# Three rearrangements in a hybrid scan, attention and feed-forward kernel: load order at the start, place of the sums and bias of the first blocks, and where an output product is cut

## The chip, the cores and the metric

The kernel runs on one core of a Trainium2 chip. The metric is the device time of one execution in microseconds (us); lower is better. Several executions are timed and their median is compared. One more execution is recorded by the hardware profiler; its own time lies beside those of the timed runs, and its rows are what the text below reads. A core has five engines that run side by side, each with its own queue of instructions: TensorE (PE in the profile, with PEld for its weight loads), VectorE (DVE), ScalarE (ACT), GpSimd (POOL) and SyncE (SP). They wait for each other through semaphores. Sixteen DMA engines move data; they are fed by queues of SP, ACT and POOL.

## What is computed

The input `x` is 2 sequences of 2048 rows of 256 floats. Four residual stages follow one another, each on normalised rows:

```python
x = x + attn_a(_layernorm(x))   # a gated scan over time
x = x + ffn(_layernorm(x))
x = x + attn_b(_layernorm(x))   # a second-order linear attention, 16 heads of 64
x = x + ffn(_layernorm(x))      # the same weights as the first feed-forward part
```

`attn_a` normalises once more with a gain `gamma`, multiplies by `w_qkva` (256 to 3 x 256: the parts q, kv and a), takes the sigmoid of a, runs `s_t = a_t * s_(t-1) + kv_t` along time, and returns `q * s`. `ffn` rounds both weight matrices to three values around a scale that is the mean of their absolute values (w + (t - w), so the result is -1, 0 or 1), and computes `gelu(x W1 + b1) W2 + b2`. `attn_b` keeps running sums over time of k k', q v' and a product of both, and ends in an output product with `W_o` (1024 to 256). All is in float32.

## The kernel before

All rows of `x` stay in SBUF for the whole kernel, as `x_sb`: 32 chunks of 128 rows. Four chunks are a block (512 rows, 512 KB), and `blocks` lists the eight blocks with the two sequences in turn, so `blocks[0]` is chunks 0 to 3 and `blocks[1]` chunks 16 to 19. The engines' orders (PE, DVE, ACT, POOL) are written out by hand: an engine issues its instructions in the order in which the Python code makes them, and waits in that order.

**Loads (L110 to L143).** SP and ACT share the four chunks of block 0, then ACT takes `gam` (1 KB, 8 bytes for each partition), and SP takes `wqkva` in three parts of 256 KB: part 2 (a), 1 (kv), 0 (q). Then SP loads block 1 (L117), the two halves of `w1` (L119), block 2 (L120), `w2` (L121), the other blocks (L123) and the attention's weights (L125). POOL's queue loads `b1_sb` (L142, 4 KB) and `b2_sb` (L143), which is one row of 1 KB copied to all 128 partitions (128 KB).

**The front (L680 to L903).** Block 0 is scanned in two units of two chunks (units 0 and 1), each further block is one unit (unit 2 is block 1). For a unit u: `s_(u)` makes the statistics of its rows on DVE (L156, L157, L165, L166) and ends them on POOL (L169, L173, L174); `r_(u)` normalises rows (L183 on DVE for units 0 and 1, L188 on ACT later); `t_(u)` turns them by PE transposes (L212) and copies with the gain on ACT (L216); `q_(u, e)` multiplies a half e of the features on PE (L334: part a, then kv, then q, one PSUM bank each), takes the sigmoid on ACT (L343), runs the scan on DVE (L353), copies the last column on POOL (L355) and multiplies by q on DVE (L357); `a_(u)` turns the result back (L433) and adds it to `x_sb` (L435). There are eight PSUM banks, taken in turn, so a product waits until the reader of the product eight banks ago is done. Between these steps the weights of the feed-forward part are rounded: `ternary_part` has two DVE instructions (L322, L323) and one on POOL (L324) for a quarter of a matrix. The first lines of the order are:

```python
s_(0, bias=False); r_(0); s_(1, bias=False); r_(1); t_(0); q_(0, 0); s_(2); t_(1); q_(0, 1)
```

Then a loop over the blocks, with index i, runs the feed-forward part of block i (`ffn_in`: L532 on PE, L544, L550 and L564 on ACT, L558 to L581 on DVE; `ffn_out`: L623, L629), and between its products the scan of a later block as seven products instead of eight (`scan_seven`: L392 on PE, L398 on DVE, L404 to L427 on ACT). `ffn_rows` on POOL (L509 to L512) makes sums that the products need. At the end of a turn i, `ffn_bias(blocks[i + 1])` adds `b2_sb` to the rows of the next block on POOL (L667), and the statistics of later blocks follow. Block 0 gets its bias at the end of turn 1.

**The attention (L913 to L1332).** It has 32 steps s (16 chunks of two sequences). In a step PE runs `inter` (L1054: queries times state), `products` (L1037, masked on DVE at L1043), the output product `outward` of an earlier step (L1115: eight matmuls into one bank; the profile counts two instructions for each), `intra` (L1068, which reads what L1043 wrote), the products that make k, q and v of the next chunks (L978, L983) and `update` (L1094). `outward(s - 2, 0)` is the last thing in step s and has the first four of its matmuls; `outward(s - 2, 1)` comes in step s + 1, between `products` and `intra`, has the other four, and DVE then adds the bank to `x_sb` (L1121). The last stage (L1451 on) is the feed-forward part once more.

## Time and profile before

| what | value |
|---|---|
| timed runs | 1212.58, 1214.03, 1215.69 us; median 1214.03 |
| the profiled execution | 1215.55 us, of it 1213.7 us from the first to the last instruction (the span) |
| granted TensorE clock | 0.999 of full |
| PE busy | 1197.3 us (99% of the span) |
| DVE, ACT, POOL busy | 818.1, 619.6, 252.3 us (67%, 51%, 21%) |
| DMA moved | 113.00 MB |
| start to 100 us, PE busy by stretch | 0 to 8.58: 5.18; 8.58 to 23.54: 14.63 of 14.96; 23.54 to 58: 34.46 of 34.46; 58 to 100: 40.85 of 42.00 us |
| 330 to 1030 us (the attention), PE busy | 693.51 of 700 us |

A row of the profile names an engine, the source line, what is written and read, and the sizes; a timeline row begins with the start and the duration in us, and ends, where the engine stood idle before it, with the idle time and what ended it. Matmuls overlap in the engine's pipeline, so two starts in a row tell more of the pace than the durations do.

### The profile page before, as it was taken

The numbers are of one execution on the slowest core, as the hardware profiler recorded it, in microseconds if no ns is written. First come the engines' busy times: TensorE is split into PE (matmuls) and PEld (weight loads), VectorE is DVE, ScalarE is ACT, GpSimd is POOL, SyncE is SP. The second block draws the span as 40 slices with busy tenths as digits, with TensorE's granted clock in tenths as the row PEclk, the third lists the DMA queues.
The fourth block names the chain that finished last, engine by engine and source line by source line (L and its number), as shares of the span: only waits on it lengthen the run. The fifth ranks groups of instructions, "written<-read, shape, count | busy, mean of one in ns | idle before, by whom it ended". The sixth has DMA issues, their size and how long they took to land.

```text
span 1213.7 us, 46646 instructions
## 1 busy us (share of the span) xinstructions
PE 1197.3 (99%) x21156; PEld 972.3 (80%) x21156; DVE 818.1 (67%) x1322; ACT 619.6 (51%) x979; POOL 252.3 (21%) x383
## 2 busy tenths in 40 slices
PE   8999999999999999999999999999999999999998
PEld 6598999999667777777778777777777889999997
DVE  7968777875567567666666656766766655676764
ACT  4356765543554554554544445445455553555542
POOL 3664335451200110110011011011011111322330
PEclk9999999999999999999999999999999999999999
DMA  9211111110244233234323323323323631212111
GB/s 319 85 61 36 35 36 35 37 56 14 88 124 135 80 125 125 91 107 134 122 82 126 123 90 125 123 92 107 124 90 107 190 96 52 70 61 79 53 52 36
DMA packets 80439, 113.00 MB, mean 93 GB/s; under 512 B 8272, under 2 KB 65360, under 8 KB 79984
## 3 DMA queue, kind: packets, MB, share of 16 engines
q1 hardware_dynamic: 77712, 105.94, 26.4%
q10 hardware_dynamic: 2448, 3.93, 1.1%
q8 instruction: 166, 2.72, 1.0%
q0 software_dynamic: 80, 0.14, 0.1%
q14 instruction: 33, 0.27, 0.1%
HBM read 58.59 MB, written 51.38 MB: 91 GB/s over the span
## 4 chain that ended last, share of the span: by engine, by line
PE 94%; DVE 2%; ACT 1%; issue 1%; POOL 1%; DMA 1%; SPq 0%; DVEq 0%; ACTq 0%; POOLq 0%
PE hy L1115 10%; PE ox L623 9%; PE hx L532 9%; PE hkN_X L983 5%; PE hp L1037 5%; PE hqT_X L978 5%; PE hvN_X L983 5%; PE oz L623 5%; PE hz L532 4%; PE huT L1068 3%; PE hS L1094 3%; PE huT L1054 3%; PE hoT L1054 3%; PE hoT L1068 3%; PE pq L334 3%; PE hM L1094 3%
## 5 line engine op out<-in xcount | busy, mean ns | idle before, releaser
L1043 DVE TENSOR_TENSOR p<-hp,mask 128x512 f32<-128x512 f32 x128 | 82.1, 682 | 96.2 <-PE hp L1037 96.2
L935 POOL TENSOR_TENSOR S<-xnT 128x128 f32<-128x128 f32 x32 | 14.8, 461 | 530.9 <-ACT xnT L280 513.2
L1115 PE MATMUL hy<-wo,oT 128*128 128x256 f32 x512 | 123.7, 385 | 0.1
L188 ACT ACTIVATE xn<-x_sb,nb,rs 128x256 f32<-128x256 f32 x124 | 65.8, 592 | 87.0 <-POOL nb L174 87.0
L1115 PEld LDWEIGHTS hy<-wo,oT 128*128 128x128 f32 x512 | 93.6, 190 | 19.2 <-issue 7.0
L544 ACT ACTIVATE hT<-hT,b_sb 128x256 f32<-128x256 f32 x192 | 85.4, 501 | 33.4 <-DVE hT L576 30.5
L1079 ACT COPY uT<-huT 128x512 f32<-128x512 f32 x32 | 18.8, 586 | 130.8 <-PE huT L1068 130.8
L1104 DVE TENSOR_TENSOR S<-S,hS 128x512 f32<-128x512 f32 x60 | 41.3, 688 | 44.5 <-PE hS L1094 41.4
L232 DVE STREAM_TRANSPOSE sqkT<-kN 128x1024 f32<-128x1024 f32 x32 | 65.8, 2058 | 1.3 <-ACT kN L1014 1.2
L1134 ACT COPY kT<-rawkT 128x1024 f32<-128x1024 f32 x32 | 66.6, 2080 | 0.0
L232 DVE STREAM_TRANSPOSE squN<-uT 128x1024 f32<-128x1024 f32 x31 | 63.6, 2051 | 4.0 <-ACT uT L1081 3.5
L1134 ACT COPY uN<-rawuN 128x1024 f32<-128x1024 f32 x31 | 64.6, 2083 | 1.6 <-DMA rawuN<-dsquN 1.2
L509 POOL TENSOR_TENSOR xT<-xnT 128x256 f32<-128x256 f32 x15 | 16.8, 1122 | 178.7 <-ACT xnT L280 118.3
L156 DVE BATCH_NORM_STATS2 st<-x_sb 128x6 f32<-128x256 f32 x128 | 51.5, 403 | 2.3 <-DMA x_sb<-in_x_dram 2.3
L1094 PEld LDWEIGHTS hS<-kN 64*64 64x64 f32 x1984 | 32.7, 134 | 23.2 <-issue 23.1
L1014 ACT COPY vN<-hvN_X 128x512 f32<-128x512 f32 x16 | 9.4, 587 | 80.0 <-PE hvN_X L983 80.0
L988 DVE TENSOR_TENSOR kN<-kN,hkN_Y 128x512 f32<-128x512 f32 x16 | 11.0, 688 | 54.7 <-ACT kN L997 54.7
L629 DVE TENSOR_TENSOR x_sb<-x_sb,ox 128x256 f32<-128x256 f32 x64 | 26.5, 414 | 30.1 <-PE ox L623 30.1
L169 POOL TENSOR_TENSOR rs<-rs,mhalf 128x2 f32<-128x2 f32 (+1 forms) x43 | 38.9, 904 | 29.4 <-DVE rs L166 26.6
L615 DVE TENSOR_TENSOR hS<-hT 128x512 f32<-128x512 f32 x62 | 41.2, 686 | 5.6 <-ACT hT L544 5.6
L334 PE MATMUL pq<-xnT,wqkva 128*128 128x512 f32 (+1 forms) x120 | 42.9, 510 | 1.4 <-DMA wqkva<-in_wqkva_t_dram 1.4
L1104 DVE TENSOR_TENSOR M<-M,hM 128x512 f32<-128x512 f32 x60 | 41.0, 684 | 4.6 <-PE hM L1094 1.4
(300 smaller groups left out, 3024.5 us busy)
## 6 DMA issues: line engine op xcount, KB each, us to landing
dsqkT<-sqkT SPq DMA_DIRECT2D x32, 512.0 KB, 3.5
rawkT<-dsqkT SPq DMA_DIRECT2D x128, 128.0 KB, 3.0
dsquN<-squN SPq DMA_DIRECT2D x31, 512.0 KB, 3.3
rawuN<-dsquN SPq DMA_DIRECT2D x124, 128.0 KB, 3.3
out_dram<-x_sb SPq DMA_DIRECT2D x16, 256.0 KB, 2.2
x_sb<-in_x_dram SPq DMA_DIRECT2D x7, 512.0 KB, 8.9
dsqxn<-sqxn SPq DMA_DIRECT2D x14, 256.0 KB, 3.7
rawxn<-dsqxn SPq DMA_DIRECT2D x56, 64.0 KB, 2.4
```

What stands on the lines that cost most here:

```text
L232: nc.vector.transpose(to, src)
L334: nc.tensor.matmul(pq[:, :nt], lhsT=wqkva[:, d, col : col + P], rhs=xnT[:, d, :], start=(d == 0), stop=(d == ND - 1),)
L532: nc.tensor.matmul(at[a][:, j, :], lhsT=A[:, f * P : (f + 1) * P], rhs=Bm, start=(new and j == 0), stop=True, skip_group_check=True,)
L544: nc.scalar.activation(out, out if src is None else src[:, j, :], AF.Gelu, bias=b1_sb[:, f : f + 1])
L623: nc.tensor.matmul(banks[name][:, c, :], lhsT=A[f // 2][:, f % 2, c * P : (c + 1) * P], rhs=Bm[:, f, :], start=(new and c == 0 and f == 0) ...
L983: nc.tensor.matmul(to, lhsT=self.A[i], rhs=self.B[i], start=new, stop=True, skip_group_check=True)
L1043: nc.vector.tensor_tensor(d[s][nm][:, h], banks[h], mask8, ALU.mult)
L1054: nc.tensor.matmul(banks[c][halves[h ^ c], p, :], lhsT=d[s][sums][c][halves[h], p, :], rhs=d[s]["qT"][halves[h], p, halves[c]], start=(p = ...
L1094: nc.tensor.matmul(banks[c][halves[h], p, :], lhsT=d[s][left][halves[c], feats(h, p)], rhs=d[s][right][halves[c], feats(h, p)], start=True ...
L1104: nc.vector.tensor_tensor(t, prev, banks[c], ALU.add)
L1115: nc.tensor.matmul(py, lhsT=d[s]["oT"][:, p, :], rhs=wo[:, p, :], start=(p == 0), stop=(p == NPR - 1),)
L1134: act(t, d[s]["r" + nm].rearrange("p t q -> p q t"))
```

## The change

There are five edits. (1) SP issues `wqkva` part 2 right after the first chunk of block 0, then the third chunk, then parts 1 and 0; ACT issues the second chunk, `gam`, and then the fourth chunk. Before, all four chunks went ahead of `gam` and `wqkva`. (2) `b2_sb` moves from POOL's queue at the start to SP's queue, behind the last rows of `x` and ahead of the attention's weights. (3) `s_(2)` stands ahead of `q_(0, 0)`: on DVE the statistics of block 1 now come before the scan of unit 0's first half; on POOL their end comes before the column copy of that scan. (4) The POOL instruction of the third quarter of `w2` (L324) is held back until `fw_(0)` (L509 to L512) has been issued, and the bias of blocks 1 and 0 is added in turn 1, after the fourth product of its `ffn_in`, in place of the ends of turns 0 and 1. (5) `outward` is cut into three and five matmuls.

```diff
     for c in range(BC):
         g = blocks[0] + c
         (nc.scalar if c % 2 else nc.sync).dma_start(out=x_sb[:, g, :], in_=xf[g * P : (g + 1) * P, :])
-    nc.scalar.dma_start(out=gam, in_=gamma)
-    for part in (2, 1, 0):
-        cols = slice(part * D, (part + 1) * D)
-        nc.sync.dma_start(out=wqkva[:, :, cols], in_=wqkva_t[:, cols].rearrange("(c p) e -> p c e", p=P))
+        if c == 1:
+            nc.scalar.dma_start(out=gam, in_=gamma)
+        if c != 1:
+            cols = slice((2, 2, 1, 0)[c] * D, ((2, 2, 1, 0)[c] + 1) * D)
+            nc.sync.dma_start(out=wqkva[:, :, cols], in_=wqkva_t[:, cols].rearrange("(c p) e -> p c e", p=P))
...
     for g0 in blocks[3:]:
         nc.sync.dma_start(out=x_sb[:, g0 : g0 + BC, :], in_=rows(xf, g0, BC))
+    nc.sync.dma_start(out=b2_sb, in_=b2.partition_broadcast(P))
...
-    nc.gpsimd.dma_start(out=b2_sb, in_=b2.partition_broadcast(P))
...
-    def ternary_part(pool, w, scale, part, name):
+    def ternary_part(pool, w, scale, part, name, later=False):
...
+        if later:
+            return lambda: nc.gpsimd.tensor_tensor(wf, wf, t, ALU.subtract)
         nc.gpsimd.tensor_tensor(wf, wf, t, ALU.subtract)
...
         t_(0)
+        s_(2)
         q_(0, 0)
-        s_(2)
         t_(1)
...
-        tern(w2, scales[2], 2)
+        rest_of = tern(w2, scales[2], 2, later=True)
         ft_(0)
         q_(4, 1)
         fw_(0)
+        rest_of()
         tern(w2, scales[2], 3)
...
                 run(squares)
                 run(steps, 2)
+                if i == 1:
+                    ffn_bias(blocks[1])
+                    ffn_bias(blocks[0])
...
-            if more:
+            if more and i > 0:
                 ffn_bias(blocks[i + 1])
-                if i == 1:
-                    ffn_bias(blocks[0])
...
-            for p in range(half * NPR // 2, (half + 1) * NPR // 2):
+            for p in range(3) if half == 0 else range(3, NPR):
```

More of the change, by code (lines that the diff above doesn't have):

```diff
@@ L720, in fw_, with tern @@
             fn[i] = ffn_rows(ffn_pool, blocks[i], fn[i])
-        def tern(w, scale, part):
-            ternary_part(tern_pool, w, scale, part, "w1" if w is w1 else "w2")
+        def tern(w, scale, part, **kw):
+            return ternary_part(tern_pool, w, scale, part, "w1" if w is w1 else "w2", **kw)
         scales = {}
```

## The prediction

> **What bounds the kernel now.** The page first: TensorE is the bound, at full clock, and every microsecond to be had is one in which it stands still.

> ```profile
> span 1213.7 us, 46646 instructions
> ...
> PE 1197.3 (99%) x21156; PEld 972.3 (80%) x21156; DVE 818.1 (67%) x1322; ACT 619.6 (51%) x979; POOL 252.3 (21%) x383
> ```

> Then PE's waits (line, what it waited for, total, times, longest):

> ```profile
> PE pq L334 <- DMA wqkva<-in_wqkva_t_dram: 1.4, 1, 1.4
> ...
> PE qax L392 <- DVE a L398: 0.8, 1, 0.8
> ...
> PE hx L532 <- POOL xT L510: 0.4, 1, 0.4
> PE hx L532 <- ACT hT L564: 0.3, 1, 0.3
> ```

> All four lie in the first 103 us, where four of the five edits are. The chain that ended last, cut to 0 to 110 us (start, us, what), says what stands behind them:

> ```profile
> 1.66 6.79 DMA wqkva<-in_wqkva_t_dram
> ...
> 14.71 1.02 POOL rs L169
> 16.87 1.58 ACT xn L188 x3
> ...
> 58.58 1.10 POOL w L324
> 59.98 0.69 POOL xT L509
> ...
> 91.58 1.41 DVE rs L165
> ```

> So: the load of part a until 8.45 us; the statistics of block 1 (end on POOL, then ACT's normalised rows); L324 ahead of L509; one small DVE instruction of 1.41 us. The change touches each. The attention has no such wait; its timeline, at one step:

> ```profile
> 572.71 0.59 ACT L1014 COPY qT<-hqT_X 128x512 f32<-128x512 f32 x1 [1.43 <-PE hqT_X L978]
> ...
> 574.33 1.16 PE L1054 MATMUL huT<-qT,S 64*64 64x64 f32 x64
> ...
> 576.36 1.99 PE L1115 MATMUL hy<-wo,oT 128*128 128x256 f32 x8
> 576.48 1.29 DVE L1043 TENSOR_TENSOR p<-hp,mask 128x512 f32<-128x512 f32 x2 [1.57 <-PE hp L1037]
> 578.28 1.31 PE L1068 MATMUL huT<-p,kN 64*64 64x64 f32 x62
> ```

> **Cutting the output product 3 and 5: nothing.** One matmul is two PE instructions 0.216 us apart, 0.43 us, moved past L1054 and L1037; no work is added. What it would cover: L1068 waits for L1043, which ends at 576.48 + 1.29 = 577.77; L1068 starts at 578.28, 0.51 us later, so there is nothing to cover. What it uncovers: L1054 starts 0.43 us earlier and needs ACT's L1014, done at 573.30; 1.03 us of room becomes 0.60. The mask's bank for L1037 has over 2 us. DVE's L1121 comes when the eighth matmul ends, as before. Bounds: a gain if the pace of these eight matmuls hides a wait (1.92 us to the next start here, 1.82 for the other half at the step's end: 0.10 x 29 steps = 3 us), against 0.43 x 30 = 13 us if the room were gone. The 0.10 sits behind the first matmul, where PE passes from 64x64 to 128x128 tiles, and that passage stays. I take 0.

> **Bias out of turn 0: 0.9 us gained.** In turn 0 POOL's L667 runs from 90.59 to 92.96; DVE's L165, 0.17 us elsewhere, starts at 91.58 and ends at 92.98, with L667. Behind it on DVE stand the two adds L398 (93.09, 93.43), and PE's fourth `qax` needs the first. Without L667 there, L165 ends at 91.75, L166 at 91.95, the adds at 92.4 and 92.7 at the latest, and PE's instruction is free when its predecessors are out: 91.88 + 4 x 0.216 = 92.74 instead of 93.66. Gain 0.92. ACT follows PE here (its L427 waits for PE), so the 0.3 us wait of L532 on L564 stays. In the new place two L667 (2.37 each) follow the norm ends of turn 0, about 99 to 104. DVE has L262, L558, L572, L576 there; other L262 beside POOL rows take 1.12 to 1.13 against 1.07 us, and L629, the first DVE add on block 1's rows, comes at 111. POOL's next work is at 113. At worst each L262 is held until an L667 ends, 1 to 2 us, and a few tenths reach PE; I take 0 for the place, 0.92 in all (0.5 to 0.95).

> **L324 behind `ffn_rows`: 0.14 us gained.** L509 now starts at 59.94, behind L324 (58.58 to 59.85). Without it the next thing in POOL's order is the column copy L355, which needs the scan L353 on DVE, 58.35 + 1.27 = 59.62. So L509 comes at 59.80, not at 58.6: 0.14. The PE wait it ends is longer, 61.85 - 60.43 - 0.86 = 0.56, and that is the upper bound. Behind it, POOL ends the w2 sums one L324 (1.25 us) later, near 71; PE reads the first of them at 73.36, 7 us after it was ready.

> **The first loads and the order of statistics and scan: 1.1 us gained.** PE's first product waits for part a until 8.58; ACT's half of `xnT` for it was ready at 7.45. With part a second on SP's queue, ahead of 512 KB that now precede it, it should be in by 4.5 to 6.8 us (below), so PE starts at 7.45, 1.13 us earlier. That gain is kept only if the next gate moves as well. On DVE block 1's statistics now stand before the first scan, and PE's unit-1 products need the bank that this scan reads; all of DVE is queued behind a transfer. Call S the start of these statistics. From the rows 11.95 to 19.92 of DVE's timeline: statistics 2.53, scan and multiply 0.79 + 0.34, the second pair the same, L290 2.31, its total 0.18, so the next scan at S + 7.28 (ACT's sigmoid for it is ready at S + 6.9); then 0.78 + 0.34 + 2.54 for block 2's statistics and 0.33 + 0.41 for the two adds L435: S + 11.7. PE's way through ACT's L188 gives the same end: those rows depend on S through POOL's L169, and 23.54 - 11.95 = 11.6. The product at 23.54 needs the second L435. Gain there: 23.54 - 11.7 = 11.85 - S. After it, to 58 us, PE is never idle and waits have 1.5 us of room, so this carries.

> S is the later of 9.57 (DVE free) and block 1's landing. Before, that was 3.52 + 8.2 = 11.7 us. Ahead of it go the same bytes but for `b2`, 128 KB. The DMA view gives 315 GB/s from 2.5 to 4 us, 166 from 4 to 6, 229 from 6 to 8, and 375 from 8 to 12. The dip is in the stretch in which `gam`'s 128 packets of 8 bytes and then `b2`'s packets of 4 KB run. [...] By the row, 6 to 8 us moved 0.46 MB in 2 us; without b2's 0.13 MB and at 375 GB/s the rest takes 0.88 us: 1.1 us sooner, S = 10.6, gain 1.25. I take S = 10.75, nearer to the row, since the neighbouring stretch shows that rate: gain 1.1, range 0.3 (`gam`'s dip grows, as now a row chunk stands behind it) to 2.2 (S = 9.6).

> The fourth chunk's wait: behind `gam` on ACT's queue. `gam` came 2.4 us after the last chunk before (6.7 against 4.3), so the chunk lands near 3.5 + 2.4 + 0.5 = 6.4 us, 7.4 at the late end; DVE wants it at 7.02. Even 7.4 moves only `r_(1)`, which ends at 9.57 and would end at 9.95, still before S. Behind it SP's second `w1` load is issued near 6.5, not 4.7 (it reuses `gam`'s semaphore); L290 needs it only at S + 4.8 = 15.5, and it landed at 14.3. On POOL the issue of `b2` (0.58 us at 2.72) goes away, ahead of 1.2 us of idle time: nothing; the column copy L355 now comes behind the statistics' end at S + 4.4, and the scan that reads it at S + 7.3. `b2` itself is needed at 99 us; the attention's weights behind it, 0.4 us later, after 300.

> **Sum.** 1.1 + 0.14 + 0.92 + 0 = 2.2 us off the profiled 1213.7 us span (1215.55 us with 1.8 around it). The median of the timed runs is 1.5 us under that execution; the difference is applied to it: 1214.03 - 2.2 = 1211.8 us, 0.18% faster. A measurement of this kernel tells about 0.3% (3.6 us) from no change; the three runs differ by 3.1.

> **Rivals.**
> 1. *The load moves but its successors don't* (20%): block 1 lands at 11.7 as before, because bytes and `gam` set it. The 1.13 us of the earlier start is handed back at the bank wait; what stays is 0.14 + 0.92: 1213.0. [...] Against: the dip at 6 to 8 us.
> 2. *The transfers come smoothly* (10%): S = 9.6 gives 2.25, with the full 0.56 at L510 and 0.92: 3.7 us, 1210.3. Against it: `gam` keeps its place early.
> 3. *The 0.10 us per step in front of L1068 is a wait that the extra matmul hides* (5%): 3 us more, 1208.8. Against: the room of 0.51 us.
> 4. *Slower: cover lost ahead of L1054* (6%). ACT's L1014 must be 0.60 us later than in the step shown before PE waits at all, and about 0.8 us later in all 30 steps (0.2 x 30 = 6 us, less the 2.2) to be slower by 0.3%; at the full 0.43: 1214.0 - 2.2 + 12.9 = 1224.7. Against: the same 1.03 us recurs in all steps, and ACT is busy for half of the span.

> The forecast as summed has 59%.

> **How the numbers follow.** Rivals 1 and the forecast, and half of 2, lie within 0.3%: 84% with rounding. Faster by over 0.3%: half of 2 and rival 3, 10%. Slower: rival 4, 6%. The range holds rivals 1 and 2 and the scatter of a median (about 1 us each way) round them: 1209.0 to 1215.0; 3 and 4 are left out.

> **What would show it.** Right: PE's first L334 at 7.4 to 7.6 us with no DMA wait; DVE's four L156 of block 1 directly behind L183, after an idle spell that a DMA ends, at 10 to 11.4; PE's L334 of unit 2 near 22.4; L165 at 0.17 us and no wait of `qax` on L398; L510 still PE's releaser; the start of L1068 after L1043's end by 0.95 instead of 0.51 us, and the step of 43.3 us per pair unchanged. Wrong: an L183 or L156 held for the fourth chunk past 8 us, a PE wait on L1014, an L262 of over 2 us beside L667.

## The result, and the profile after

The changed kernel takes 1209.08 us (median of 6, 1207.8 to 1209.94), beside 1214.07 us for the kernel before on the same chip (6 runs): ratio 0.9957, 95% interval 0.9944 to 0.997. In 1214 us that is 5.2 us, 3.6 to 6.8. The forecast was 2.2 us. The profiled execution of the changed kernel took 1209.94 us, with a span of 1208.1 us, 5.6 us shorter than before.

The added lines shift the numbering: L334 is now L337, L392 is L395, L398 is L401, L510 is L513, L532 is L535, L1014 is L1019, L1037 is L1042, L1043 is L1048, L1054 is L1059, L1068 is L1073, L1094 is L1099, L1115 is L1120. The page of the changed kernel:

```profile
span 1208.1 us, 46645 instructions
PE 1196.3 (99%) x21156; PEld 972.3 (80%) x21156; DVE 817.7 (68%) x1322; ACT 618.9 (51%) x979; POOL 251.0 (21%) x382
```

TensorE is still the bound. Its waits after the change (line, what it waited for, total, times, longest):

```profile
PE huT L1073 <- issue: 1.1, 2, 0.7
...
PE hM L1099 <- issue: 0.6, 1, 0.6
...
PE pq L337 <- ACT xnT L217: 0.3, 1, 0.3
PE hx L535 <- ACT hT L567: 0.3, 1, 0.3
PE hx L535 <- POOL xT L513: 0.3, 1, 0.3
...
PE hp L1042 <- issue: 0.2, 1, 0.2
```

Of the four waits that the prediction showed, the one for the load is gone (PE now waits 0.3 us for ACT's rows), the one for the small DVE instruction is gone, and the two of L535 stay. But the same view of the kernel before has other rows, which the prediction left out:

```profile
PE hoT L1068 <- issue: 1.4, 4, 0.5
...
PE huT L1068 <- issue: 1.0, 2, 0.7
...
PE hp L1037 <- issue: 0.5, 1, 0.5
...
PE hM L1094 <- issue: 0.2, 1, 0.2
```

"issue" is idle time for which the profile shows no wait. The largest row, `hoT` in `intra`, is gone after the change.

Where the gain lies follows from the starts of the same PE instructions in both profiled executions: 0.91 us at the first product of the scan (8.58 to 7.67), 1.58 at the products of unit 2 (23.54 to 21.97), 1.66 behind L324 and the column sums, 2.58 behind the bias (93.66 to 91.08), 2.65 at 294 us. In the attention it goes up in jumps of 0.2 to 0.7 us and down in jumps of up to 0.4, and is 5.64 at 1092 us. So some 2.6 us come from the first 100 us, where 2.2 were forecast, and 3.0 us from the attention, where nothing was.

A part of the 2.6 us is scatter of the one profile before. There part a of `wqkva` landed at 8.45 us. In two kernels of the experiments that keep the old order of loads (the cut alone and the bias alone) it landed at 6.51 and 6.96 us, and the first product started at 7.61 and 7.63 us, as early as in the changed kernel. PE's wait for this load in these two:

```profile
PE pq L334 <- DMA wqkva<-in_wqkva_t_dram: 0.6, 1, 0.6
```

```profile
PE pq L334 <- DMA wqkva<-in_wqkva_t_dram: 0.4, 1, 0.4
```

So the 0.91 us are not shown to be the change's. Those two gain 0.22 and 0.41 us at the products of unit 2, so that of the 1.58 us there some 1.2 to 1.4 are left for the change.

One step of the attention after the change (start, duration, then at the end the idle time before and what ended it):

```profile
570.07 0.59 ACT L1019 COPY qT<-hqT_X 128x512 f32<-128x512 f32 x1 [1.43 <-PE hqT_X L983]
...
571.26 1.16 PE L1059 MATMUL huT<-qT,S 64*64 64x64 f32 x64
...
573.28 2.42 PE L1120 MATMUL hy<-wo,oT 128*128 128x256 f32 x10
573.41 1.29 DVE L1048 TENSOR_TENSOR p<-hp,mask 128x512 f32<-128x512 f32 x2 [1.11 <-PE hp L1042]
...
575.64 1.16 PE L1073 MATMUL huT<-p,kN 64*64 64x64 f32 x64
```

This is as forecast: L1059 still has 0.60 us of room behind ACT's L1019 (570.66 to 571.26), and L1073 starts 0.94 us after the mask's end (574.70). From the start of L1120 to that of L1073 it was 1.92 us with eight instructions and is 2.36 with ten: exactly one matmul more. Nothing is gained here. In the attention the gain comes in some steps only, inside the runs of small matmuls.

### The profile page after: what moved, and what is told of

It is laid out like the page before. It is cut to its first block, busy times and chain, and to the rows that moved or that the text cites. A ratio compares the mean times of both kernels' runs of the same rounds, so it can differ in the third digit from the quotient of the medians.

```text
span 1208.1 us, 46645 instructions
## 1 busy us (share of the span) xinstructions
PE 1196.3 (99%) x21156; PEld 972.3 (80%) x21156; DVE 817.7 (68%) x1322; ACT 618.9 (51%) x979; POOL 251.0 (21%) x382
## 3 DMA queue, kind: packets, MB, share of 16 engines
q8 instruction: 166, 2.72, 0.9%
## 4 chain that ended last, share of the span: by engine, by line
PE 95%; DVE 1%; ACT 1%; issue 1%; DMA 1%; POOL 0%; SPq 0%; ACTq 0%; DVEq 0%; POOLq 0%
PE ox L626 10%; PE hy L1120 9%; PE hx L535 9%; PE hkN_X L988 5%; PE hqT_X L983 5%; PE hp L1042 5%; PE hvN_X L988 5%; PE oz L626 5%; PE hz L535 5%; PE pq L337 3%; PE huT L1073 3%; PE hS L1099 3%; PE huT L1059 3%; PE hoT L1059 3%; PE hM L1099 3%; PE hoT L1073 2%
## 5 line engine op out<-in xcount | busy, mean ns | idle before, releaser
L1048 DVE TENSOR_TENSOR p<-hp,mask 128x512 f32<-128x512 f32 x128 | 82.2, 683 | 82.9 <-PE hp L1042 82.9
L1120 PE MATMUL hy<-wo,oT 128*128 128x256 f32 x512 | 123.6, 385 | 0.0
L1120 PEld LDWEIGHTS hy<-wo,oT 128*128 128x128 f32 x512 | 93.7, 190 | 18.9 <-issue 6.7
L512 POOL TENSOR_TENSOR xT<-xnT 128x256 f32<-128x256 f32 x15 | 16.4, 1094 | 179.8 <-ACT xnT L281 118.7
L1099 PEld LDWEIGHTS hS<-kN 64*64 64x64 f32 x1984 | 32.7, 134 | 23.2 <-issue 23.1
L1019 ACT COPY vN<-hvN_X 128x512 f32<-128x512 f32 x16 | 9.4, 586 | 80.1 <-PE hvN_X L988 80.1
L1073 PEld LDWEIGHTS huT<-p,kN 64*64 64x64 f32 x2048 | 33.5, 134 | 13.0 <-issue 7.1
## 6 DMA issues: line engine op xcount, KB each, us to landing
out_dram<-x_sb SPq DMA_DIRECT2D x16, 256.0 KB, 2.2
dsqxn<-sqxn SPq DMA_DIRECT2D x14, 256.0 KB, 3.9
```

What stands on the lines that cost most here:

```text
L1048: nc.vector.tensor_tensor(d[s][nm][:, h], banks[h], mask8, ALU.mult)
L1073: nc.tensor.matmul(banks[c][halves[h ^ c], p, :], lhsT=d[s][nat][halves[c], feats(h, p)], rhs=d[s][pm][halves[c], h, p, :], start=(d[s][su ...
L1099: nc.tensor.matmul(banks[c][halves[h], p, :], lhsT=d[s][left][halves[c], feats(h, p)], rhs=d[s][right][halves[c], feats(h, p)], start=True ...
L1120: nc.tensor.matmul(py, lhsT=d[s]["oT"][:, p, :], rhs=wo[:, p, :], start=(p == 0), stop=(p == NPR - 1),)
```

## The experiments

Two theories. A: PE now and then stands still inside its runs of 64x64 matmuls because its own instruction stream comes late, and the slow matmul that the change moves ahead of `intra` gives that stream time. B: the cut is worth nothing, as predicted; such standstills fall by chance, and the shorter front moved them.

A standstill is counted here where two 64x64 matmuls that follow each other in the trace start over 0.12 us apart, between 330 and 1030 us; the usual distance is 0.02 us (62 in 1.31 us). One of 0.30 us near 360 us stands at the same place of the program in every kernel, also in those below that shift PE's stream; it is left out of all counts.

**The cut alone.**

```diff
-            for p in range(half * NPR // 2, (half + 1) * NPR // 2):
+            for p in range(3) if half == 0 else range(3, NPR):
```

> The kernel before with the cut of the output product in three and five matmuls, and nothing else. Theory A (PE's own instruction stream runs short in the stretches of small matmuls, and a slow matmul more ahead of `intra` lets it fill up): about 2.5 us faster than before, and between 370 and 960 us about half as many standstills inside runs of 64x64 matmuls as before (10 with 4.5 us there, 5 with 1.8 us in the changed kernel). Theory B (the cut is worth nothing, as predicted; the standstills only fall elsewhere because the front has become 2.6 us shorter): the same as before within 0.5 us, about 10 standstills.

1211.38 us beside 1214.05: ratio 0.9979 (0.997 to 0.9987), 2.5 us faster. 4 standstills with 3.1 us, before 12 with 6.0. Theory B falls: the front is as before here, and the time moved by more than its 0.5 us. The same place in both, first the kernel before, then this one, PE alone:

```profile
706.44 1.99 PE L1115 MATMUL hy<-wo,oT 128*128 128x256 f32 x8
708.36 1.16 PE L1068 MATMUL huT<-p,kN 64*64 64x64 f32 x64
709.35 0.39 PE L1068 MATMUL hoT<-p,vN 64*64 64x64 f32 x10
710.07 1.04 PE L1068 MATMUL hoT<-p,vN 64*64 64x64 f32 x54 [0.33 <-issue]
```

```profile
706.61 1.16 PE L1068 MATMUL huT<-p,kN 64*64 64x64 f32 x64
707.59 1.11 PE L1068 MATMUL hoT<-p,vN 64*64 64x64 f32 x64
```

Before, the run of 64 is torn after ten matmuls, with "issue" as the cause; with the new cut it runs through. (The 0.33 us of the row count from the end of the row before, 709.35 + 0.39; the starts of the two matmuls are 0.55 us apart.)

**The changed kernel with four and four again.**

```diff
-            for p in range(3) if half == 0 else range(3, NPR):
+            for p in range(half * NPR // 2, (half + 1) * NPR // 2):
```

> The changed kernel with the output product cut in four and four, as before. Theory A: about 2.5 us slower than the changed kernel (1211.6 us), with about 10 standstills between 370 and 960 us. Theory B: the changed kernel's time, 1209.1 us, with its 5 standstills.

1210.80 us, ratio 0.9973 (0.9962 to 0.9983): 3.3 us of the 5.2 are left, so the cut is worth about 1.9 us here (the interval overlaps that of the change, 0.9944 to 0.997). 10 standstills with 4.2 us, as A has it.

**The bias alone.**

```diff
                 run(steps, 2)
+                if i == 1:
+                    ffn_bias(blocks[1])
+                    ffn_bias(blocks[0])
...
-            if more:
+            if more and i > 0:
                 ffn_bias(blocks[i + 1])
-                if i == 1:
-                    ffn_bias(blocks[0])
```

> The kernel before with only the bias of blocks 1 and 0 moved into turn 1. The prediction's step: 0.92 us faster. In the profile the small DVE instruction ahead of the adds of the fourth scan product takes 0.17 instead of 1.41 us. Theory A and B alike: 0.9 us faster (1213.1 us) and about 10 standstills between 370 and 960 us; a difference of more than 1.5 us to the time before would speak for theory B, that any shift of the front changes the standstills later on.

1212.35 us, ratio 0.9989 (0.998 to 0.9998): 1.3 us, 0.2 to 2.4. L165 takes 0.17 us, and at the fourth `qax` the trace gains 0.92 us, to the hundredth what was summed. 10 standstills with 4.8 us: a front that is shorter by 0.9 us does not take them away.

**Loads, output bias and statistics alone** (the first two hunks of the change, the moved line of `b2_sb`, and `s_(2)` ahead of `q_(0, 0)`).

> The kernel before with only the new order of the first loads, the load of the output bias behind the rows, and the statistics of block 1 ahead of the first scan. From the trace of the changed kernel: PE's first product of the scan 0.9 us earlier, the products of unit 2 1.6 us earlier. Theory A: 1.6 us faster in all (1212.5 us), about 10 standstills between 370 and 960 us. Theory B: some other number of them, and a gain that differs from 1.6 us by up to 2 us either way. The prediction as it stood: 1.1 us.

1212.27 us, ratio 0.9985 (0.9975 to 0.9995): 1.8 us, 0.6 to 3.0. Behind 60 us the trace shows 1.59 us. 14 standstills with 6.5 us, so again it is not the front that removes them.

**Where the standstills are.** The page of the kernel before counts a queue of the kind "instruction":

```profile
q8 instruction: 166, 2.72, 1.0%
```

166 packets of 16 KB (2.72 MB in all). PE has 21156 matmuls and as many weight loads, 42312 instructions, and the trace holds 188 semaphore and drain rows of it besides: 42500 for 166 packets, 256.0 each, so the queue is taken to be PE's, with 256 instructions in a packet. Counted over all these rows, the 12 standstills of the kernel before lie whole multiples of 256 rows apart, to within one. The records of the trace, counted from PE's first instruction, say at which instruction each standstill ends. Worked out from them: number of the packet, start and end of its transfer, start of its first instruction (us), and the distance to the instruction before:

```
before       91   701.77  703.04   705.63   0.04
before       92   707.82  708.78   710.07   0.55
before       93   711.62  712.99   714.80   0.00
cut alone    92   704.29  705.71   707.71   0.04
```

A packet's first instruction runs about 2.2 us after the start of the transfer at the earliest. Packet 92 of the kernel before was wanted sooner: without the standstill of 0.55 us it would have had 1.7. With the new cut the same packet has 3.4 us, and nothing stands. One matmul lasts 0.43 us, so most of the 1.7 us more comes from an earlier start of the transfer (167 instead of 152 instructions ahead of the packet), and why it started earlier is not shown. Over all packets whose first instruction lies in `hoT`, between 330 and 1030 us, the median time from the start of the transfer is 2.6 us in the five profiled executions with four and four and 3.1 us in the eight with three and five.

Three shifts test whether the packets are what counts: small matmuls in place of large ones in the warm-up move all of PE's later instructions by 64, 128 or 192 places in its stream and leave the rest of the program as it is.

```diff
-        for _ in range(12):
+        for _ in range(8):
             nc.tensor.matmul(warm, lhsT=ones, rhs=ones, start=True, stop=True)
+        for _ in range(20):
+            nc.tensor.matmul(warm[:CH, :CH], lhsT=ones[:CH, :CH], rhs=ones[:CH, :CH], start=True, stop=True)
```

(8 and 20; 4 and 40; 1 and 59.)

> The changed kernel with PE's warm-up at the start made of 8 large and 20 small matmuls instead of 12 large ones: 64 PE instructions more (48 + 64), about the same time, and from there on every instruction of PE stands 64 places later in PE's stream. Theory A, made sharper by the first runs: PE's stream comes in packets of 16 KB, 256 instructions each, and PE stands still at the first instruction of a packet when it gets there less than about 2.3 to 2.7 us after that packet's transfer began. Then all standstills inside runs of 64x64 matmuls between 330 and 1030 us (9 with 3.8 us in the changed kernel) move: where one comes back at the same boundary, it stands 64 instructions earlier in the program. Their number and sum change, between 1 and 8 us in all, and the time with them (1207 to 1213 us). Theory B (no tie to the packets): the same places in the program, and 1209.1 us but for what the warm-up itself changes in the first 10 us.

> The same with 4 large and 40 small warm-up matmuls: PE's stream 128 places later. Theory A: standstills 128 instructions earlier in the program, other number and sum, 1207 to 1213 us. Theory B: as the changed kernel, 1209.1 us, with its standstills in their places.

> The same with 1 large and 59 small warm-up matmuls: PE's stream 192 places later. Theory A: standstills 192 instructions earlier in the program, other number and sum, 1207 to 1213 us. Theory B: as the changed kernel, 1209.1 us, with its standstills in their places.

The times, 1207.76, 1215.53 and 1218.85 us beside 1212.76 (ratios 0.9969, 1.0037, 1.0057), say little: the small matmuls took 0.11 us per PE matmul instead of the few hundredths assumed, and in the profiled executions PE began its first transposes 2.8, 5.3 and 8.1 us later. The timed runs of the first shift lie in two groups, 1206.3 to 1208.6 and 1210.7 to 1212.3, and its profiled execution is of the second, so only its attention is read. There the result is plain: 2, 5 and 5 standstills with 0.7, 1.6 and 4.0 us, at other places. Packet 141, for one, begins with instruction 36405 of the stream in the first and the second shift, as in a later kernel without a shift; it is in `huT` with a shift and in `hoT` without, and PE stands there in all three. Over all 14 profiled executions there are 97 standstills. They fall on 36 different packets. 20 of these hold PE up in more than one execution, and each does so at the same place of PE's stream every time, with a shift or without. From packet to packet the place moves on by just under 256 matmuls and weight loads. Every standstill ends 2.2 to 3.1 us (median 2.4) after the start of that packet's transfer, 1.2 to 1.7 us after its end. Theory A is shown in its sharp form: PE stands at a packet's first instruction when it gets there too soon after the start of that packet's transfer.

**Two and six.**

```diff
-            for p in range(3) if half == 0 else range(3, NPR):
+            for p in range(2) if half == 0 else range(2, NPR):
```

> The changed kernel with the output product cut in two and six matmuls. Theory A: one more slow matmul (0.43 us) stands between the start of a packet's transfer and the packet's first instruction where that lies in `intra`, and one less where it lies in `products` or in the update of M: of the standstills left in `intra` those of up to 0.43 us go, the longer ones shrink; 1208 to 1209 us. Theory B: 1209.1 us.

1207.94 us, ratio 0.9965 (0.9953 to 0.9977), beside 0.9957 of the change: not told apart. 4 standstills with 2.4 us.

**The shift by 64 with a warm-up of the old length, and the cut undone in it.** The small matmuls use two quarters of `ones` and two of `warm` in turn; they now start 0.05 us apart on average, where those of the first shift started 0.11 apart.

```diff
-        for _ in range(12):
+        for _ in range(6):
             nc.tensor.matmul(warm, lhsT=ones, rhs=ones, start=True, stop=True)
+        for k in range(22):
+            r = slice(k % 2 * CH, (k % 2 + 1) * CH)
+            nc.tensor.matmul(warm[r, :CH], lhsT=ones[r, r], rhs=ones[r, :CH], start=True, stop=True)
```

> The changed kernel with a warm-up of 6 large and 22 small matmuls, the small ones on two quarters of the array in turn: PE's stream 64 places later as in the first shift, but with a warm-up that should end about when it did (5.2 us by 6 x 0.46 and 44 passes of about 0.057). Theory A: between 330 and 1030 us the standstills of that shift, two with about 0.7 us instead of eight with 3.5 us, so 2 to 3 us faster than the changed kernel: about 1206.5 us beside a kernel before of 1214. Theory B: as the changed kernel, 5 us faster than before.

> The same with the output product cut in four and four again. If the cut is worth 2 to 3 us wherever the packets' boundaries fall: that much slower than the shifted kernel, with about ten standstills. If its worth is a matter of where they fall (theory A in its sharper form): another worth, and as the shift leaves only two standstills under the cut in three and five, between 0 and 4 us; each standstill at a boundary again.

With three and five 1207.51 us beside 1213.77, ratio 0.9947 (0.9935 to 0.996), the lowest of all; its interval overlaps that of the change (0.9944 to 0.997), so it is not shown to be faster. 4 standstills with 1.4 us, not 2 with 0.7. With four and four 1209.13 us, ratio 0.9962 (0.9949 to 0.9974), 1.8 us slower (again with intervals that overlap), 8 standstills with 3.6 us. So the cut was worth about as much with the packets beginning elsewhere. The waits of the latter have `hoT` at their head again:

```profile
PE hoT L1073 <- issue: 1.8, 3, 1.0
```

**All executions together.** The attention's length, from the first to the last small product of `hS` (L1094), is independent of the front. In the groups of the trace it is the last pair of times in the row; the kernel before, then the cut alone:

```profile
L1094 PE MATMUL hS<-kN x1984: 218/218/267, 318.9 to 980.5; 64*64 64x64 f32 x199
```

```profile
L1094 PE MATMUL hS<-kN x1984: 218/218/267, 318.7 to 976.4; 64*64 64x64 f32 x199
```

| cut | profiled executions | attention, us | standstills in `intra`, us | elsewhere, us |
|---|---|---|---|---|
| 4 and 4 | 5 | 659.8 to 662.0, mean 660.9 | 3.3 to 5.4, mean 4.0 | mean 1.0 |
| 3 and 5 | 8 | 657.0 to 659.4, mean 657.9 | 0.6 to 2.4, mean 1.6 | mean 1.1 |
| 2 and 6 | 1 | 657.1 | 1.5 | 0.9 |

Every execution with four and four is longer than every one with three and five. The 3.0 us between the means are 2.4 us of standstills in `intra`, where the moved matmul stands ahead, nothing in the other runs of small matmuls, and 0.6 us that this count does not catch.

**The load of the output bias at the start again.**

```diff
-    nc.sync.dma_start(out=b2_sb, in_=b2.partition_broadcast(P))
...
     nc.gpsimd.dma_start(out=b1_sb, in_=b1)
+    nc.gpsimd.dma_start(out=b2_sb, in_=b2.partition_broadcast(P))
```

> The changed kernel with the load of the output bias (128 KB) back on POOL's queue at the start. [...] By the prediction's row of the slow stretch: it lands 1.1 us later, at 11.2, the statistics start there and the products of unit 2 at 22.9: 0.9 us slower.

1210.29 us beside 1213.77, ratio 0.9976 (0.9965 to 0.9987), about 2.3 us slower than the change by the ratios. Block 1 lands at 11.48 us, in the changed kernel at 10.11. Over all profiled executions: 11.33 to 11.76 us in the four with this load at the start, 8.43 to 10.11 in the ten with it behind the rows. That is the row's 1.1 us and more, not the 0.35 us that the bytes alone would take (128 KB at the 375 GB/s of 8 to 12 us, an estimate). The queues of the kernel before, from 6 to 8 us, show where the time goes (packets, MB, share of the 16 engines' time; packets overlap):

```profile
q0 software_dynamic: 43, 0.12, 50.7%
q1 hardware_dynamic: 340, 0.33, 49.0%
```

The first is POOL's queue, with a quarter of the bytes and half of the packets' time. The load is 32 packets of 4 KB there, which took 0.53 us each on average, where the 4 KB packets of SP's queue up to 16 us took 0.16. Why they are slower on POOL's queue at this time is not shown. At the products of unit 2 this kernel keeps only 0.36 us of the change's 1.58, within the 0.22 and 0.41 us of the two kernels with the old order: without the new place of `b2` the other edits at the front add nothing there that shows.

DVE's statistics of block 1 and PE's products of unit 2, here and then in the changed kernel:

```profile
11.50 0.43 DVE L157 BATCH_NORM_STATS2 st<-x_sb 128x6 f32<-128x256 f32 x1 [1.96 <-DMA x_sb<-in_x_dram]
...
23.18 1.55 PE L337 MATMUL pq<-xnT,wqkva 128*128 128x512 f32 x3
```

```profile
10.29 0.42 DVE L157 BATCH_NORM_STATS2 st<-x_sb 128x6 f32<-128x256 f32 x1
...
21.97 2.84 PE L337 MATMUL pq<-xnT,wqkva 128*128 128x512 f32 x6
```

Both times 11.68 us lie between the two rows: the 11.7 of the prediction's chain.

**The statistics behind the scan again.**

```diff
         t_(0)
-        s_(2)
         q_(0, 0)
+        s_(2)
```

> The changed kernel with the statistics of block 1 behind the first scan again. By the prediction's chain (the product of unit 2 follows the start of these statistics by 11.7 us): the scan and its multiplication go first on DVE, from about 10.3 to 11.4, the statistics start at 11.4 and the products of unit 2 at about 23.1 instead of 21.97: 1.1 us slower than the changed kernel. Rival: the order does not matter, as PE has room there: the same time.

1209.51 us, ratio 0.9967 (0.9954 to 0.9981): 1.2 us more than the change by the ratios, with intervals that overlap. In this execution the loads came earlier, the statistics began at 10.89, not 11.4, and the products of unit 2 at 22.41, 0.44 us later than in the changed kernel. The expected direction, less than half of the size in the trace.

## Why the prediction was wrong

**The step that failed is "Cutting the output product 3 and 5: nothing".** Its rows were right: the mask was ready 0.51 us ahead of L1068, L1054 kept its room, the passage from 64x64 to 128x128 tiles stayed where it was (in the step shown the second matmul of L1115, and of L1120 after the change, starts 0.32 us after the first, the next ones 0.22 apart). The conclusion "so there is nothing to cover" took the waits that have a releaser for all waits. PE's own supply of instructions is a second thing that it waits for here, beside the semaphores (12 standstills with 6.0 us in the kernel before), and the sentence "the attention has no such wait" passed over the "issue" rows of the very view that it quotes. 64 matmuls of `intra` take 0.99 us from start to start, and the 128 of a packet that holds nothing else about 2.0 us, while a packet needed at least about 2.2 us from the start of its transfer. One matmul of the output product takes 4 of the 256 places and 0.43 us, so a packet whose first instruction lies in `intra` has more time with one more of them ahead (the median for `hoT` went from 2.6 to 3.1 us). Measured: 1.8 to 2.5 us by the timed runs (two pairs, and the cut alone), 3.0 us by the traces.

Rival 3 had the size, 3 us, and not the cause. It named the 0.10 us per step in front of L1068; these are still there in the step shown (2.36 us with ten instructions, against 1.92 + 0.43). That the measured time comes so close to its 1208.8 us, and that it lies inside the stated range at its low end, is luck: the range was made for the front's rivals and scatter, not for a gain in the attention.

**The first loads and the order: right in mechanism, 1.1 us forecast, 1.58 measured between the two profiles, of which 0.2 to 0.4 are scatter.** The mis-sized term is S: 10.75 was taken, 10.29 measured, and 11.85 - 10.29 = 1.56. The 0.15 us by which 10.75 lies behind the row's 10.6 were the author's estimate, and no run shows them: the runs showed 10.29 in the changed kernel, and 9.55 where the loads came sooner. PE's earlier first product (1.13 us forecast) set nothing by itself, as the prediction had it: the next gate did. The row was right, and too small: moving the 128 KB of `b2` brought block 1 forward by 1.4 us in the pair of profiles, against the row's 1.1 and the 0.35 of its bytes, and by 2.1 us between the means of all (11.5 and 9.5). A second term ran against it: the last two chunks of block 0 came at 7.17 and 7.34 us, the late end that was allowed for, which held DVE's rows of unit 1 until 10.29; so at the end DVE and not the load set S (block 1 was there at 10.11). Where the loads came sooner, as in the shift with the warm-up of the old length, S was 9.55 and the products of unit 2 started at 21.57: rival 2, the smooth transfers, is what some executions do.

**The bias, 0.92 us: right**, in the whole change and alone. Its new place costs nothing that shows: POOL's two additions run from 96.8 to 101.5 us, and PE's gain stays 2.6 us behind them.

**L324, 0.14 us: 0.08 measured**, and L513 is still what releases PE there.

**Of the cases,** the slower one is out: the one wait of L1059 for ACT, 0.7 us, is in both kernels. The front's 2.6 us alone would have given 1211.5 us; the 2.5 us of the cut alone make it 1209.0, where 1209.1 was measured.

## What to carry to other kernels

Where PE runs long stretches of small matmuls, count "issue" among its waits and ask how long a packet of its instruction stream lasts: here 256 instructions of 64x64 matmuls lasted 2.0 us and a packet's first instruction ran 2.2 us after the start of its transfer at the earliest, so moving one large matmul per step ahead of the longest run of small ones paid 2 to 3 us with no change in work. A wait with a releaser can be costed by its rows; one without needs its places compared over several executions before it is called nothing. At the start of this kernel, a small load delayed the large one behind it by more than its bytes: 128 KB on POOL's queue cost 1.4 us here, where the bytes alone would be 0.35 us at the 375 GB/s of 8 to 12 us. And one profile of a start is not enough to price a load: a wait of 1.4 us for part a was 0.4 and 0.6 us in two other executions with the same order.

## What was not expected of the hardware

The number of standstills scatters from one program to another with the same attention: 3 to 8 with 1.4 to 4.2 us among the three-and-five kernels whose warm-up was not much longer. A single profile therefore tells such an effect only to about 1.5 us.

Landing times at the start scatter as well: the last chunks of block 0 landed at 7.2 and 7.3 us in the changed kernel's profile and at 5.9 and 6.1 in that of the shift with the warm-up of the old length, with the same order of loads.
